# Selections of a Mamba scan by pairs of groups, four at once in four row tiles

## The chip, the core and the metric

The kernel runs on one core of one Trainium2 chip. The metric is the device time of one execution in microseconds (us); lower is better. A core has a matrix engine (PE), whose weight loads are a row of their own (PEld), a vector engine (DVE), an activation engine (ACT), a general engine (POOL) and a queue that starts transfers (SP). PE writes its results to PSUM, eight banks of 128 partitions by 512 float32. Everything here is float32, and the profile records each float32 matmul as two passes: two weight loads and two matmuls.

## The reference, cut to what matters

An image batch `x` of shape (4, 56, 56, 128) passes through four layers: windowed attention, a Mamba stage, an additive attention with a token-choosing expert layer, and a full attention with an expert layer. The change touches only the Mamba stage. It runs twice in a row (two blocks `l`) over each image row, a sequence of 56 tokens:

```python
xz = h @ in_w                          # 128 -> 512, split into u and res
u  = silu(causal_conv(u) + cb)         # 4 taps
dt, Bm, Cm = split(u @ xw)             # 8, 16, 16
delta = softplus(dt @ dtw + dtb)       # 256 channels
h_t = exp(delta * A) * h_{t-1} + delta * u * Bm      # 256 channels x 16 states
y_t = sum over states of h_t * Cm, plus u * D
out = (y * silu(res)) @ ow
```

## The kernel before, in words

The Mamba stage is `layer1`. It works in 56 blocks: 4 images, 7 chunks of 8 image rows (`CH` = 448 tokens), 2 layers `l`. A block has 256 channels with 16 states each, so 4096 recurrences; a group of 8 channels fills 128 partitions, and a block has 32 groups.

For each group `g` these steps are issued, on four engines:

- `decays(g)`: a matmul picks the 8 channels out of `delta`, repeats each over 16 states and scales by A (line 545). The operand is a half of 64 rows, so two such matmuls can lie in the array. The result is a PSUM tile `a` (three buffers), and ACT takes its exponential in place (line 548).
- `inputs(g)`: the same for `du` = delta * u with `pick` (line 555), into PSUM tile `u` (two buffers).
- `scan(g)`: DVE multiplies `u` by the spread B (`dBu`, line 562), then runs the recurrence along the 448 tokens into `hs` (line 566). After each odd group POOL multiplies the pair of `hs` by the spread C (`bc`), 128 x 896 (line 570).
- `sums(g)`: after every fourth group, four matmuls with 32 columns each add up the states into `y` (line 582). With the first of a half, a matmul with a diagonal of D begins `y` (line 577).

`gate(j, f)` multiplies a finished half of `y` by `silu(res)` (DVE, line 590); `project(j)` multiplies by `ow` (lines 598 and 611) and either copies the result to the next layer's `h` (ACT, line 604) or adds it to `x` (DVE, line 616).

While block j is scanned, `mamba_pre` issues the steps of block j+1, each after a given group: the convolution as 4 matmuls for each half (line 665) and its silu (line 672), the `res` matmuls (678) and their silu (685), `xproj` (691), a copy `dbl` (697), four `spread` matmuls (702), the softplus in parts on ACT, DVE and POOL (lines 711 to 736), and `du` on POOL (740). Their PSUM tile is `m` (two buffers).

The order is written out by hand: the context holds a manual schedule for PE, ACT, DVE and POOL, so every engine runs its instructions in the order in which Python issues them, and waits only for what its next instruction needs. The main loop is

```python
for g in range(GROUPS * len(order) + GROUPS // 2):
    ...
    scan(g)
    decays(g + 2)
    inputs(g + 1)
    if i % 4 == 3: sums(g - 7)
    if i == 4: gate(j - 1, 1)
    if i == 5: project(j - 1)
    if i == 20: gate(j, 0)
    for at, step in todo: ...   # steps of block j + 1 due after group i
```

Of the kernel before, what the change touches and what calls it, by code (L numbers as in the profile page):

```python
# [10 lines left out]
AF = mybir.ActivationFunctionType  # L11
ALU = mybir.AluOpType
AX = mybir.AxisListType
PSUM = bass.MemoryType.PSUM
# [3 lines left out]
B, HW, C = 4, 56, 128  # L18
S = HW * HW
P = 128  # L20
# [3 lines left out]
CH = TC * TP  # L24
# [12 lines left out]
QG, HR = 8, 64  # L37
GROUPS = DI // 8
# [18 lines left out]
def host_constants():  # L57

    j = np.arange(HW)
    start = np.clip(j - NB, 0, HW - KW)  # L60
    kj = j[:, None]
    inside = (kj >= start[None, :]) & (kj < start[None, :] + KW)
    toep = np.zeros((1 + KR, HW, HW), np.float32)
    toep[0] = np.where(inside, 0.0, NEG)
    for d in range(KR):
        toep[1 + d] = inside & (kj - j[None, :] + KW - 1 == d)
    group = np.kron(np.eye(32), np.full((4, 4), 0.25)).astype(np.float32)
    later = np.triu(np.ones((TP, TP), np.float32), 1)
    p = np.arange(P)
    place = np.zeros((P, QW + QW - JG), np.float32)  # L70
    place[p, QW - JG + p // AH] = 1.0


    pick = np.zeros((P, QG, P), np.float32)
    back = np.zeros((P, 4, HD), np.float32)
    for q in range(QG):
        pick[:, q, :] = (p % HR // 8 == q)[:, None] & (p[None, :] // DS == p[:, None] % 8)
    for q in range(4):
        back[p, q, 8 * q + p // DS] = 1.0
    return {  # L80
        "k_state": (p[None, :] % DS == np.arange(DS)[:, None]).astype(np.float32),
        "k_pick": pick.reshape(P, QG * P),
        "k_sum": back.reshape(P, 4 * HD),
        "k_toep": toep.reshape(1 + KR, HW * HW),
        "k_group": group,
        "k_later": later,
        "k_place": place,
    }


class Hybrid:
# [336 lines left out]

    def layer1_weights(self, wp):
# [15 lines left out]
        w["sum"] = self.load(wp, [P, 4, HD], "sum", a["k_sum"].rearrange("p (q c) -> p q c", q=4))  # L445
# [51 lines left out]
    def layer1(self):  # L497
# [5 lines left out]
        with ExitStack() as ctx:  # L503
# [4 lines left out]
            ps_m = ctx.enter_context(tc.tile_pool(name="l1_m", bufs=2, space=PSUM))  # L508
            ps_a = ctx.enter_context(tc.tile_pool(name="l1_a", bufs=3, space=PSUM))
            ps_u = ctx.enter_context(tc.tile_pool(name="l1_u", bufs=2, space=PSUM))  # L510
# [11 lines left out]
            ]  # L522
            h = {}
            pre, yg, A, U, HS, py = {}, {}, {}, {}, {}, {}
# [8 lines left out]
            def select(g):  # L533
                j, i = divmod(g, GROUPS)
                if j >= len(order):
                    return None
                half = slice(i % 2 * HR, (i % 2 + 1) * HR)
                return j, order[j][2], i // 16, i // 4 % 4 + 4 * (i // 2 % 2), half

            def decays(g):  # L540
                s = select(g)
                if s:
                    j, l, f, q, own = s
                    A[g] = self.t(ps_a, [P, 512], "a")[:, :CH]
                    nc.tensor.matmul(  # L545
                        A[g], w["A"][own, l, f, q, :], pre[j]["delta"][own, f], start=True, stop=True
                    )
                    nc.scalar.activation(A[g], A[g], AF.Exp)  # L548

            def inputs(g):  # L550
                s = select(g)
                if s:
                    j, l, f, q, own = s
                    U[g] = self.t(ps_u, [P, 512], "u")[:, :CH]
                    nc.tensor.matmul(  # L555
                        U[g], w["pick"][own, q, :], pre[j]["du"][own, f], start=True, stop=True
                    )

            def scan(g):
                j = g // GROUPS  # L560
                dBu = self.t(sm, [P, CH], "dBu")
                nc.vector.tensor_mul(dBu, U.pop(g), pre[j]["bc"][:, 0])  # L562
                if g % 2 == 0:
                    HS[g // 2] = self.t(sm, [P, 2, CH], "hs", bufs=6)
                hs = HS[g // 2]
                nc.vector.tensor_tensor_scan(  # L566
                    hs[:, g % 2], A.pop(g), dBu, 0.0, op0=ALU.mult, op1=ALU.add
                )
                if g % 2:
                    nc.gpsimd.tensor_mul(hs, hs, pre[j]["bc"][:, 1:2].to_broadcast([P, 2, CH]))  # L570

            def sums(g):

                j, l, f, q, _ = select(g)
                if q == 0:
                    py[j, f] = self.t(ps_y, [P, 512], "y")[:, :CH]
                    nc.tensor.matmul(
                        py[j, f], w["Dd"][:, l, f, :], pre[j]["us"][:, f], start=True, stop=False
                    )
                for r in range(4):  # L580
                    at = r % 2 * HR + r // 2 * HD
                    nc.tensor.matmul(  # L582
                        py[j, f][at : at + HD, :], w["sum"][:, q, :], HS[(g + r) // 2][:, r % 2],
                        start=False, stop=(q == 3),
                    )
# [36 lines left out]
            decays(0)  # L622
            decays(1)
            inputs(0)
            for g in range(GROUPS * len(order) + GROUPS // 2):
                j, i = divmod(g, GROUPS)
# [7 lines left out]
                if j < len(order):  # L634
                    scan(g)
                decays(g + 2)
                inputs(g + 1)
                if i % 4 == 3 and 0 <= g - 7 < GROUPS * len(order):
                    sums(g - 7)
                if i == 4 and j:  # L640
                    gate(j - 1, 1)
                if i == 5 and j:
                    project(j - 1)
                    pre.pop(j - 1)
                if i == 20 and j < len(order):
                    gate(j, 0)
                for at, step in todo:
                    if at == i:
                        step()

    def mamba_pre(self, pre, j, block, h, w, sm, m):
# [8 lines left out]
        def conv(f, k):  # L660
            if (f, k) == (0, 0):
                r["us"] = self.t(sm, [P, NHALF, CH], "us")
            if k == 0:
                ps[f] = m()[:, :CH]
            nc.tensor.matmul(  # L665
                seqs(ps[f]), w["in"][:, l, k, f * P : (f + 1) * P], h[b, c, l][:, :, k : k + HW],
                start=(k == 0), stop=(k == DC - 1),
            )

        def silu_u():  # L670
            for f in range(NHALF):
                nc.scalar.activation(r["us"][:, f], ps[f], AF.Silu, bias=w["cb"][:, l, f : f + 1])

        def res(f):
            if f == 0:
                r["sres"] = self.t(sm, [P, NHALF, CH], "sres")
            ps[f] = m()[:, :CH]
            nc.tensor.matmul(
                seqs(ps[f]), w["res"][:, l, f * P : (f + 1) * P], h[b, c, l][:, :, DC - 1 :],
                start=True, stop=True,  # L680
            )

        def silu_res():
            for f in range(NHALF):
                nc.scalar.activation(r["sres"][:, f], ps[f], AF.Silu)
# [13 lines left out]
        def spread(i):  # L699
            own = slice(i * HD, (i + 1) * HD)  # L700
            ps[i] = m()[:, :CH]
            nc.tensor.matmul(ps[i], w["dbl"][own, l, :], r["dbl"][own, :], start=True, stop=True)
# [3 lines left out]
        def parts():  # L706
            r["e"] = self.t(sm, [P, NHALF, CH], "sp_e", bufs=1)
            r["delta"] = self.t(sm, [P, NHALF, CH], "delta")
            for f in range(NHALF):
                dtb = w["dtb"][:, l, f : f + 1]  # L710
                nc.scalar.activation(r["e"][:, f], ps[f], AF.Abs, bias=dtb)
                nc.vector.tensor_scalar(r["delta"][:, f], ps[f], dtb, 0.0, op0=ALU.add, op1=ALU.max)
            nc.scalar.activation(r["e"], r["e"], AF.Exp, scale=-1.0)

        def copy_bc():
            r["bc"] = self.t(sm, [P, 2, CH], "bc")
            for i in range(2):
                nc.scalar.copy(r["bc"][:, i], ps[2 + i])
# [19 lines left out]
        def du():  # L738
            r["du"] = self.t(sm, [P, NHALF, CH], "du")
            nc.gpsimd.tensor_mul(r["du"], r["delta"], r["us"])  # L740
# [4 lines left out]
        steps = [(2 * i // 3, conv, i // DC, i % DC) for i in range(2 * DC)]  # L745
        steps += [
            (6, silu_u), (7, res, 0), (8, res, 1), (9, silu_res), (10, xproj, 0), (11, xproj, 1),
            (12, copy_dbl), (13, spread, 0), (13, spread, 1), (14, parts), (15, spread, 2),
            (15, spread, 3), (16, copy_bc), (16, one_plus), (17, log), (18, low), (20, log1p), (22, delta), (24, du),
# [405 lines left out]
```

## Time and profile before

| | us |
|---|---|
| median of 3 runs (11249.28 to 11265.89) | 11265.24 |
| the profiled execution | 11265.46 |
| its span, first to last instruction | 11263.7 |
| the Mamba scans, first to last start | 1097.8 to 4991.0 |
| PE busy in the span | 9968.8 (89%) |
| ACT busy | 6235.4 (55%) |
| DVE busy | 4399.8 (39%) |
| POOL busy | 2404.3 (21%) |
| PE busy, DVE busy in 3000 to 3500 | 412.81, 400.16 |
| granted PE clock: mean of the span; 3000 to 3500 | 0.933; 0.96 |

The scans take 3893 us, about 69.5 us for each of the 56 blocks. In that stage POOL is busy 291 to 298 us of 500 and ACT 231 to 239. Busy time of PE counts a stretch once in which several matmuls lie in the array, and the ends of matmuls are modelled, so it overstates how full PE is. The granted clock is what the throttle let PE have: 1.00 is full speed.

### The profile page before, as it was taken

To read this page: it belongs to the slowest core of one execution; us is meant where nothing else is said; L and a number is where in the kernel's file an instruction comes from. 1 tells how busy PE (TensorE), PEld (TensorE's weight loads), DVE (VectorE), ACT (ScalarE), POOL (GpSimd) and SP (SyncE) were. 2 spreads that over 40 slices of the span, in tenths; PEclk is the share of its full clock that TensorE was granted. 3 is DMA by queue.
4 is the path that set the end of the run, shared out by engine and by line. 5 is a ranking of instruction groups with operands and counts; after the bars stand their busy time and mean duration, and the time that the engine had idled before them with its cause. 6 is when DMAs were issued, how large, how long until landed. Compare 5 with 4: busy or idle time off the path is not lost.

```text
span 11263.7 us, 117588 instructions
## 1 busy us (share of the span) xinstructions
PE 9968.8 (89%) x45951; PEld 4111.7 (37%) x45951; DVE 4399.8 (39%) x8342; ACT 6235.4 (55%) x10930; POOL 2404.3 (21%) x1422
## 2 busy tenths in 40 slices
PE   7887888888888888879999999999999789898998
PEld 3443222222222222223333333333333387565655
DVE  3444877788788877880000000000000301304133
ACT  2222444444444444439998998999899502232322
POOL 0000655556565656640000000000000000000000
PEclk8887999999999999999999999999999758999999
DMA  1000000000000000000000000000000030000000
GB/s 38 1 1 10 1 1 1 1 1 1 1 1 1 1 1 1 1 1 1 1 1 1 1 1 1 1 1 1 1 1 1 16 105 3 6 1 6 1 6 6
DMA packets 90722, 61.48 MB, mean 5 GB/s; under 512 B 20635, under 2 KB 81587, under 8 KB 89971
## 3 DMA queue, kind: packets, MB, share of 16 engines
q1 hardware_dynamic: 90165, 53.96, 1.7%
q8 instruction: 361, 5.91, 0.2%
q14 instruction: 196, 1.61, 0.0%
HBM read 46.87 MB, written 7.07 MB: 5 GB/s over the span
## 4 chain that ended last, share of the span: by engine, by line
PE 75%; DVE 13%; ACT 9%; issue 2%; SPq 0%; POOL 0%; DMA 0%; DVEq 0%; ACTq 0%; POOLq 0%
PE s L833 26%; PE a L545 9%; PE o L1033 7%; PE s L1026 5%; DVE hs L566 5%; PE o L842 4%; PE m L665 3%; PE y L582 3%; DVE dBu L562 2%; ACT e L838 2%; PE d L408 2%; PE o L408 2%; PE s L391 2%; PE s L1103 1%; ACT a L548 1%
## 5 line engine op out<-in xcount | busy, mean ns | idle before, releaser
L828 ACT ACTIVATE th<-fT,g 128x448 f32<-128x448 f32 (+3 forms) x6272 | 3327.8, 621 | 17.6 <-DVE g L809 17.5
L833 PE MATMUL s<-th,place 128*32 128x448 f32 (+4 forms) x12544 | 3181.7, 516 | 7.0 <-ACT th L828 7.0
L545 PE MATMUL a<-delta,A_pick 64*128 64x448 f32 x3584 | 1878.7, 615 | 608.8 <-DVE hs L566 591.7
L570 POOL TENSOR_TENSOR hs<-hs,bc 128x896 f32<-128x896 f32 x896 | 1860.8, 2081 | 1409.4 <-DVE hs L566 1257.4
L548 ACT ACTIVATE a<-a 128x448 f32<-128x448 f32 x1792 | 936.3, 529 | 2024.1 <-PE u L555 1908.5
L566 DVE TENSOR_TENSOR_SCAN hs<-a,dBu 128x448 f32<-128x448 f32 x1792 | 1954.5, 1091 | 232.3 <-ACT a L548 30.2
L853 DVE TENSOR_SCALAR den<-o 112x1 f32<-112x1 f32 x224 | 31.8, 152 | 4961.3 <-PE o L842 3642.2
L555 PE MATMUL u<-du,pick 64*128 64x448 f32 x3584 | 1877.6, 615 | 0.0
L833 PEld LDWEIGHTS s<-th,place 128*32 128x32 f32 (+1 forms) x12544 | 787.1, 106 | 2129.8 <-ACT th L828 2030.4
L562 DVE TENSOR_TENSOR dBu<-u,bc 128x448 f32<-128x448 f32 x1792 | 1092.9, 610 | 430.6 <-PE u L555 420.9
L545 PEld LDWEIGHTS a<-delta,A_pick 64*128 64x128 f32 x3584 | 565.8, 193 | 1780.2 <-DVE hs L566 1246.8
L1031 ACT ACTIVATE e<-s,shift 112x448 f32<-112x448 f32 x784 | 495.4, 633 | 888.6 <-PE s L1026 840.4
L840 POOL TENSOR_TENSOR e<-e,later 112x112 f32<-112x112 f32 x112 | 47.2, 421 | 3813.8 <-ACT e L838 3813.8
L1033 PEld LDWEIGHTS o<-xa,e 112*112 112x112 f32 x6272 | 711.1, 176 | 297.7 <-ACT e L1031 295.5
L1033 PE MATMUL o<-xa,e 112*112 112x129 f32 x6272 | 789.3, 279 | 13.4 <-ACT e L1031 0.9
L1026 PE MATMUL s<-xT 128*112 128x448 f32 x1568 | 656.2, 541 | 0.0
L842 PE MATMUL o<-xa,e 112*112 112x129 f32 x3248 | 492.3, 288 | 105.9 <-ACT e L838 98.6
L555 PEld LDWEIGHTS u<-du,pick 64*128 64x128 f32 x3584 | 565.9, 193 | 54.4 <-issue 53.4
L842 PEld LDWEIGHTS o<-xa,e 112*112 112x112 f32 x3248 | 384.5, 176 | 446.7 <-ACT e L838 402.7
L396 ACT ACTIVATE e<-s 112x896 f32<-112x896 f32 (+1 forms) x272 | 206.2, 800 | 590.6 <-PE s L391 427.5
L582 PE MATMUL y<-hs,sum 128*32 128x448 f32 x3584 | 462.7, 589 | 4.0 <-POOL hs L570 4.0
L758 POOL MEMSET xa<- 112x28 f32 x12 | 1.6, 148 | 1823.6 <-DVE X L856 1281.6
(224 smaller groups left out, 8064.9 us busy)
## 6 DMA issues: line engine op xcount, KB each, us to landing
w<-in_L_ffn_weight SPq DMA_DIRECT2D x16, 1024.0 KB
w<-in_L_ffn_weight SPq DMA_DIRECT2D x64, 256.0 KB
X<-in_x SPq DMA_DIRECT2D x8, 784.0 KB
out<-X SPq DMA_DIRECT2D x8, 784.0 KB
e_edge<-dtab SPq DMA_DIRECT2D x42, 49.0 KB
cw<-in_L_conv_conv_w SPq DMA_DIRECT2D x1, 1024.0 KB
e_inner<-dtab SPq DMA_DIRECT2D x14, 49.0 KB
dtab<-tab SPq DMA_DIRECT2D x1, 637.0 KB
```

The source lines that it names most:

```text
L545: nc.tensor.matmul(A[g], w["A"][own, l, f, q, :], pre[j]["delta"][own, f], start=True, stop=True)
L548: nc.scalar.activation(A[g], A[g], AF.Exp)
L555: nc.tensor.matmul(U[g], w["pick"][own, q, :], pre[j]["du"][own, f], start=True, stop=True)
L562: nc.vector.tensor_mul(dBu, U.pop(g), pre[j]["bc"][:, 0])
L566: nc.vector.tensor_tensor_scan(hs[:, g % 2], A.pop(g), dBu, 0.0, op0=ALU.mult, op1=ALU.add)
L570: nc.gpsimd.tensor_mul(hs, hs, pre[j]["bc"][:, 1:2].to_broadcast([P, 2, CH]))
L582: nc.tensor.matmul(py[j, f][at : at + HD, :], w["sum"][:, q, :], HS[(g + r) // 2][:, r % 2], start=False, stop=(q == 3),)
L828: nc.scalar.activation(th[:, lo:], fT[:, c * CH + lo : (c + 1) * CH], AF.Tanh, bias=g[:, at : at + 1])
L833: nc.tensor.matmul(ps[QW * blk : QW * blk + rows, lo:CH], place[:, off : off + rows], th[:, lo:], start=(q == 0), stop=(n + 1 == NG or q = ...
L842: nc.tensor.matmul(po[s][:TP, : C + 1], e[:, s * TP : (s + 1) * TP], xa[:, J, :], start=(J == 0), stop=(J == TC * c + s),)
L1026: nc.tensor.matmul(ps[:TP, :CH], xT[:, t * TP : (t + 1) * TP], xT[:, c * CH : (c + 1) * CH], start=True, stop=True,)
L1033: nc.tensor.matmul(po[s][:TP, : C + 1], e[:, s * TP : (s + 1) * TP], xa[:, t, :], start=(t == 0), stop=(t == NT - 1),)
```

## The change

Two groups become a pair `p`, 16 pairs to a block.

- `select(p)` issues four matmuls one after the other, each on 32 rows: two for `a` (two groups, from `delta`) and two for `u` (from `du`). So that the four lie in four different row tiles, the halves of `du` are stored swapped: POOL writes `du` as two products over 64 partitions each.
- `a` and `u` are two banks each. `a` has two buffers (4 banks), `u` one (2), `m` one, `y` one: the eight banks.
- ACT takes one exponential over 128 x 896, DVE one product `dBu` over 128 x 896.
- DVE's order is: first scan of pair p, product of pair p+1, second scan of pair p.
- `sums` runs for two pairs at a time; the diagonal matmul is a step of its own, `skip`; `gate`, `project` and `skip` follow each other after pair 2, `gate` and `skip` after pair 10.
- `mamba_pre`: the convolution and `res` results are copied by ACT to a tile `raw`, and one silu over 128 x 1792 replaces four; `spread` evacuates each tile at once; the steps of a pair are issued half after `select`, half at the end.

```diff
-            ps_m = ctx.enter_context(tc.tile_pool(name="l1_m", bufs=2, space=PSUM))
-            ps_a = ctx.enter_context(tc.tile_pool(name="l1_a", bufs=3, space=PSUM))
-            ps_u = ctx.enter_context(tc.tile_pool(name="l1_u", bufs=2, space=PSUM))
+            ps_m = ctx.enter_context(tc.tile_pool(name="l1_m", bufs=1, space=PSUM))
+            ps_a = ctx.enter_context(tc.tile_pool(name="l1_a", bufs=2, space=PSUM))
+            ps_u = ctx.enter_context(tc.tile_pool(name="l1_u", bufs=1, space=PSUM))
...
+            def place(p):
+                j, i = divmod(p, PAIRS)
+                return j, i // 8, i // 2 % 4, i % 2 * 2
+
+            def select(p):
+                if p >= n_pairs:
+                    return
+                j, f, q, r0 = place(p)
+                l = order[j][2]
+                A[p] = self.t(ps_a, [P, 2, 512], "a")[:, :, :CH]
+                U[p] = self.t(ps_u, [P, 2, 512], "u")[:, :, :CH]
+                for k in range(2):
+                    own = slice((r0 + k) * HD, (r0 + k + 1) * HD)
                     nc.tensor.matmul(
+                        A[p][:, k], w["A"][own, l, f, q, :], pre[j]["delta"][own, f],
+                        start=True, stop=True,
+                    )
+                for k in range(2):
+                    r = (r0 + k + 2) % 4
+                    own = slice(r * HD, (r + 1) * HD)
                     nc.tensor.matmul(
+                        U[p][:, k], w["pick"][own, q, :], pre[j]["du"][own, f], start=True, stop=True
+                    )
+                nc.scalar.activation(A[p], A[p], AF.Exp)
+
+            def inputs(p):
+                if p < n_pairs:
+                    V[p] = self.t(sm, [P, 2, CH], "dBu")
+                    nc.vector.tensor_mul(
+                        V[p], U.pop(p), pre[p // PAIRS]["bc"][:, 0:1].to_broadcast([P, 2, CH])
+                    )
+
+            def scan(p, k):
+                if k == 0:
+                    HS[p] = self.t(sm, [P, 2, CH], "hs", bufs=5)
                 nc.vector.tensor_tensor_scan(
+                    HS[p][:, k], A[p][:, k], V[p][:, k], 0.0, op0=ALU.mult, op1=ALU.add
+                )
...
-                if j < len(order):
-                    scan(g)
-                decays(g + 2)
-                inputs(g + 1)
-                if i % 4 == 3 and 0 <= g - 7 < GROUPS * len(order):
-                    sums(g - 7)
-                if i == 4 and j:
+                now = [x for x in todo if x[0] // 2 == i]
+                if p < n_pairs:
+                    scan(p, 0)
+                select(p + 1)
+                for _, step in now[: len(now) // 2]:
+                    step()
+                inputs(p + 1)
+                if p < n_pairs:
+                    scan(p, 1)
+                    weigh(p)
+                if i % 2 and 0 <= p - 3 < n_pairs:
+                    sums(p - 3)
+                if i == 2 and j:
                     gate(j - 1, 1)
-                if i == 5 and j:
                     project(j - 1)
                     pre.pop(j - 1)
-                if i == 20 and j < len(order):
+                if i == 2 and j < len(order):
+                    skip(j, 0)
+                if i == 10 and j < len(order):
                     gate(j, 0)
+                    skip(j, 1)
+                for _, step in now[len(now) // 2 :]:
+                    step()
...
+        def silu():
+            act = self.t(sm, [P, 2 * NHALF, CH], "act")
+            r["us"], r["sres"] = act[:, 0:NHALF], act[:, NHALF:]
+            nc.scalar.activation(act, r["raw"], AF.Silu)
...
             r["du"] = self.t(sm, [P, NHALF, CH], "du")
-            nc.gpsimd.tensor_mul(r["du"], r["delta"], r["us"])
+            for k in range(2):
+                to, of = slice(k * 64, k * 64 + 64), slice(64 - k * 64, 128 - k * 64)
+                nc.gpsimd.tensor_mul(r["du"][to], r["delta"][of], r["us"][of])
...
-        steps = [(2 * i // 3, conv, i // DC, i % DC) for i in range(2 * DC)]
+        steps = [(2 * i // 3, project, i // DC, i % DC) for i in range(2 * DC)]
         steps += [
-            (6, silu_u), (7, res, 0), (8, res, 1), (9, silu_res), (10, xproj, 0), (11, xproj, 1),
-            (12, copy_dbl), (13, spread, 0), (13, spread, 1), (14, parts), (15, spread, 2),
-            (15, spread, 3), (16, copy_bc), (16, one_plus), (17, log), (18, low), (20, log1p), (22, delta), (24, du),
+            (6, project, 2, 0), (7, project, 3, 0), (8, silu), (9, xproj, 0), (10, xproj, 1),
+            (11, copy_dbl), (12, spread, 0), (13, spread, 1), (14, exp), (15, one_plus),
+            (16, log), (17, low), (18, spread, 2), (19, spread, 3), (19, log1p), (21, delta), (23, du),
         ]
```

In the new `mamba_pre`, `project(f, k)` is the convolution's tap k of half f (f below 2) or the `res` matmul (f of 2 and 3), followed by ACT's copy to `raw` when the tile is whole. `spread(i)` for i below 2 is followed at once by ACT's absolute value and by DVE's `tensor_scalar` (the line 712 of before), for i of 2 and 3 by ACT's copy to `bc`.

## The prediction

> **What bounds the kernel now.** First the windows by stage: of 500 us in the scans PE is busy 413 and DVE 400, so neither is full.
>
> ```profile
> 3000.00:3500.00 500.00, 412.81 (x1734) 130.03 (x1732) 400.16 (x496) 238.41 (x378) 297.37 (x162) 0.97 0.00 1
> ```
>
> (PE, PEld, DVE, ACT, POOL, granted clock.) Then the groups by line in that window, for durations and what ended idle time:
>
> ```profile
> L566 DVE TENSOR_TENSOR_SCAN hs<-a,dBu 128x448 f32<-128x448 f32 x232 | 253.0, 1091 | 30.4 <-ACT a L548 3.6 <-DVE dBu L562 1.0 <-ACT sp_ln L726 0.5
> L545 PE MATMUL a<-delta,A_pick 64*128 64x448 f32 x464 | 239.8, 606 | 73.8 <-DVE hs L566 73.1
> L562 DVE TENSOR_TENSOR dBu<-u,bc 128x448 f32<-128x448 f32 x232 | 141.5, 610 | 55.8 <-PE u L555 54.6
> ```
>
> PE waits for scans to free `a`, DVE for `u`: a ring between two engines. Scan starts in the trace lie 1.71 to 1.74 us apart where DVE alone limits; the median plain block takes 68.5 us, so some 13 of it are waits and other DVE work. The timeline gives one turn of the ring at full clock, then one at half:
>
> ```profile
> 2511.33 0.64 PE L545 MATMUL a<-delta,A_pick 64*128 64x448 f32 x1
> 2511.33 0.64 PE L555 MATMUL u<-du,pick 64*128 64x448 f32 x1
> 2511.81 0.54 PE L545 MATMUL a<-delta,A_pick 64*128 64x448 f32 x1
> 2512.42 0.62 DVE L562 TENSOR_TENSOR dBu<-u,bc 128x448 f32<-128x448 f32 x1
> ```
> ```profile
> 2528.45 1.11 PE L555 MATMUL u<-du,pick 64*128 64x448 f32 x1
> 2529.35 0.95 PE L555 MATMUL u<-du,pick 64*128 64x448 f32 x1
> 2530.38 0.62 DVE L562 TENSOR_TENSOR dBu<-u,bc 128x448 f32<-128x448 f32 x1 [0.28 <-PE u L555]
> ```
>
> From selection to product: 1.10 us at full clock, 1.94 at half. The clock changes in steps of 3.41 us; windows of that length show when:
>
> ```profile
> 2736.67:2740.09 3.42, 2.70 (x18) 0.76 (x16) 3.21 (x4) 3.38 (x4) 1.60 (x1) 1.00 0.02 5
> 2740.09:2743.50 3.41, 1.61 (x8) 0.30 (x4) 2.81 (x4) 2.65 (x5) 2.07 (x2) 1.00 0.01 2
> 2743.50:2746.91 3.41, 2.94 (x8) 1.01 (x8) 2.92 (x5) 0.53 (x1) 3.41 (x2) 0.50 0.00 0
> 2746.91:2750.33 3.42, 3.42 (x12) 0.70 (x10) 2.46 (x3) 0.53 (x1) 3.42 (x3) 0.50 0.01 2
> 2750.33:2753.74 3.41, 2.22 (x14) 0.79 (x10) 1.87 (x3) 1.06 (x2) 3.41 (x3) 1.00 0.00 0
> ```
>
> PE is busy 1.61 of 3.41: the next window has half clock. 2.94 doesn't end that, 3.42 does. I cut the whole scan stage so: of 67 full-clock windows with PE busy under half, 66 were followed by half clock; of 971 above, 12. Of 79 half-clock windows busy over 0.9, 77 were followed by full clock; of 23 below, 1. Before, 9% of windows are at half clock.
>
> **The parts.** *Four in the array.* A selection with what follows holds PE 0.94 us (starts 2510.377 back to 2509.424 and the like). Whether four row tiles run together, layer 0 shows: four 32-row score matmuls (line 391) start at 94.915, 94.921, 94.935 and 94.941, and second passes follow 0.42 later. So four cost 0.94, like two; per block PE sheds 16 x 0.94 = 15 us. [...]
>
> *DVE.* Two products of 0.599 become one of 896: from 0.467 at 0.96 elements/ns and 0.132 fixed, 1.07 us (bounds 0.95 and 1.22, two whole ones: 16 x 0.12 to 0.15 = 2 us a block). A product followed by its own scan has the scan 0.70 to 0.73 later, though it lasts 0.60; a scan lets the next go after 1.01. Alternated, nothing follows its own input, so DVE alone would need 1.01 + 0.98 + 1.01 = 3.00 for a pair, against 2 x 1.72 = 3.44.
>
> *The ring.* `a` has two buffers of a pair, so selection p+1 waits for the second scan of p-1, and product p+1 follows it in the same pair. A pair costs 1.10 (selection to product) + 0.98 (product) + 1.09 (second scan) + 0.05 (semaphore, 2512.34 to 2512.39) = 3.22; the first scan lies under the selection. At half clock 4.06. Sixteen pairs: 51.5.
>
> *What lies between.* PE is in order, so what is issued in a pair beyond its 3.22 delays the next selection. Durations: a matmul between others 0.95, following one of its kind 0.75, `sums` 0.89, `project` 1.93 or 1.70.
> - Pairs 0 and 1, convolution: 0.94 + 2.45 = 3.39, and 0.94 + 0.95 + 0.89 + 1.70 = 4.48: +1.4.
> - Pair 2: `gate` 0.65, `project` 2.04 until `x` can be added, 0.69, `skip` 0.95, convolution 0.75, all before the next selection, with one `y` bank: 5.1 in place of 0.13: +5.0 (+4.6 where ACT copies `h`). Next scan, product and exponential are queued behind it. Pair 3, `res`: +0.5.
> - Pair 4: `xproj` waits for the silu, and selection 6 behind it: 1.06 to the exponential, 0.95, table 1.28, silu 1.80 (0.951 + 2 x 0.42, from the 448 and 896 rows), 0.95: 6.0 against 3.22: +2.8.
> - Pairs 6 and 7: two `delta` operations on DVE 1.2 and a wait for `spread` 0.7: +1.9.
> - Pairs 8 and 9: exponential, table, log, identity, table, exponential (1.06 + 0.95 + 1.28 + 0.95 + 0.94 + 1.28 + 0.95), `bc` copy 0.54, `spread` 0.95 for the one `m` bank: 9.0 against 6.4: +2.5.
> - Pair 10: `gate` and `skip`: +1.5.
>
> Sum 15.4; the block 67.0 at full clock, 1.5 below 68.5. Costed at nothing: two table loads fewer (6 to 4) and four copies more, since ACT is busy 238 of 500; the two `du` products on POOL, 1.04 to 2.08 us each (2.08 for 896 columns): queued behind `weigh` they end some 3 us before selection 16 and the sums of pair 15 need POOL's results, and if that cover is gone cost at most 2.08 x 56 = 116 us; three image changes (84 to 86 us blocks) with one `m` bank, 0 to 3 x 16 = 48 us, nearer 0 as DVE does most of that work.
>
> *The clock.* A plain pair now holds PE 1.03 (recorded span of a selection) and every second pair 0.96 more: 0.32 to 0.62 of 3.22, mostly under a half where before it was 1.03 of 1.71. At half clock it is about 0.7 of 4.06, under the 0.9 that ends it. Charges per block:
> - pairs 11 to 15: 5 x 0.84, a quarter off for windows that happen to return: 3.2;
> - pairs 0 and 1 begin at half clock and need one dense window, some 5 us, in which half the work is lost: 2.5, take 2.0;
> - PE idles 4 us for the silu; then `xproj`, selection, `xproj`, `sums` at half: 2.9, take 2.5;
> - pair 8 has only a selection: 1.1 in pairs 9 and 10; the `gate` wait of pair 2: 0.5.
>
> 9.3 in all (13.4 with every charge in full), so 76.3 a block, 7.8 over 68.5. The granted clock of the stage falls from 0.95 to about 0.77. [...]
>
> **Sum.** Profiled 11265.5 (span 11263.7 and 1.8 around it; the median is 11265.24): + 56 x 7.8 = 437: 11,702, say 11,700. With half the charges 71.6 a block: 11,440; with all in full 80.4: 11,930.
>
> **Rivals.** *The clock stays (faster).* If four tiles at once count as more activity than two, or selections fall so that windows hold over half, the block is 67.0: 56 x 1.5 = 84 less, 11,181; with the 0.95 product 11,080. It decides while charges stay under 1.5 us a block, two pairs at half clock. For it: 91% of windows are full now. Against: 66 of 67. Chance 0.17; within 0.2% (22.5 us, about what a measurement can tell) 0.05, the edge between the two.
> *Row tiles don't overlap.* If `a` and `u` pairs take turns, the selection is 0.75 longer, a pair 3.97 at full clock; PE then stays above half: 67.0 + 12 = 79.0, +588: 11,850. Against: line 391. Chance 0.06.
> *DVE's alternation gains nothing* because the ring, not DVE, sets the pair: that is in my sum. Forecast, slower by the clock: 0.72.
>
> The numbers: faster 0.17, same 0.05, slower 0.78. The likeliest case alone spans 11,440 to 11,930; the range reaches down to 11,160, into the full-clock case, since without it 0.22 and more would be left out.
>
> **What would show it.** Right: scan-stage clock 0.70 to 0.85, plain pairs 4.06 apart with selections 1.9 before their product, PE busy well under 413 of 500, 5 us without a scan after pair 2. Wrong: clock at 0.95 and pairs at 3.2 (first rival); four selections starting in two steps (second); a product far from 1.07.

## The result, and the profile after

The changed kernel takes 12010.55 us (median of 4 runs, 12006.2 to 12014.64) against 11264.95 for the kernel before (4 runs): a ratio of 1.0665, 95% interval 1.0647 to 1.0684, so 746 us slower. The prediction had the side and the mechanism, but its 11,700 was too low and its range, up to 11,930, too short. The profiled execution took 12006.2 (span 12004.4). Of the 741 us by which it is longer than the one of before, 720 lie between the first and the last scan start: 4612.8 us (1127.5 to 5740.2) in place of 3893.1. The median block is 81.9 us.

The granted clock in the page's slices (tenths of full speed, 40 slices), then the 500 us window that was shown of before (us, PE, PEld, DVE, ACT, POOL, clock, DMA, GB/s):

```profile
PEclk8887766666666666666899999999999956999999
```
```profile
3000.00:3500.00 500.00, 363.47 (x1442) 114.82 (x1434) 318.20 (x340) 184.86 (x212) 257.10 (x140) 0.68 0.00 1
```

The clock of the stage is 0.68; in the same 500 us before it was 0.97, as the row in the prediction has it. Every engine that does the stage's work does less of it in the same time: DVE runs 189 scans here, before 232. The groups by line in that window (count | busy, mean ns of one | idle before, by releaser):

```profile
L569 DVE TENSOR_TENSOR_SCAN hs<-a,dBu 128x448 f32<-128x448 f32 x189 | 197.4, 1073 | 0.5
L547 PE MATMUL a<-delta,A_pick 32*128 32x448 f32 x380 | 150.4, 847 | 66.8 <-DVE hs L569 66.0 <-DVE gn_var L189 0.7
...
L562 DVE TENSOR_TENSOR dBu<-u,bc 128x896 f32<-128x896 f32 x95 | 103.4, 1088 | 145.0 <-PE u L554 133.4 <-PE a L547 11.6
```

The scan itself no longer waits (0.5 us): DVE's idle time has moved to the product, 145.0 us in 95 turns, nearly all of it for `u`, and PE for its part waits for scans. A matmul lasts 847 ns on average, before 606. The timeline shows two turns of the ring, the first at half clock and the second at full (start, us, instruction):

```profile
3085.39 1.11 PE L547 MATMUL a<-delta,A_pick 32*128 32x448 f32 x2 [2.32 <-DVE hs L569]
...
3085.41 1.12 PE L554 MATMUL u<-du,pick 32*128 32x448 f32 x2
...
3087.35 1.09 DVE L562 TENSOR_TENSOR dBu<-u,bc 128x896 f32<-128x896 f32 x1 [1.13 <-PE u L554]
...
3088.36 2.06 DVE L569 TENSOR_TENSOR_SCAN hs<-a,dBu 128x448 f32<-128x448 f32 x2
...
3089.59 0.65 PE L547 MATMUL a<-delta,A_pick 32*128 32x448 f32 x2 [0.80 <-DVE hs L569]
...
3089.60 0.64 PE L554 MATMUL u<-du,pick 32*128 32x448 f32 x2
...
3090.70 1.09 DVE L562 TENSOR_TENSOR dBu<-u,bc 128x896 f32<-128x896 f32 x1 [0.28 <-PE u L554]
3091.71 2.06 DVE L569 TENSOR_TENSOR_SCAN hs<-a,dBu 128x448 f32<-128x448 f32 x2
...
3092.93 1.11 PE L547 MATMUL a<-delta,A_pick 32*128 32x448 f32 x2 [2.32 <-DVE hs L569]
```

All four first passes start within 0.02 us, so four row tiles do run together. From selection to product it is 1.96 us at half clock and 1.11 at full, and the turns are 4.20 (3085.39 to 3089.59) and 3.34 us long. Then the same stretch by windows of 3.41 us, with the clock behind the busy times (the cuts lie 0.2 us behind the clock's own steps, hence 0.53 and 0.97):

```profile
3081.92:3085.33 3.41, 1.16 (x8) 0.00 (x0) 2.29 (x4) 0.90 (x1) 3.33 (x2) 0.50 0.00 0
3085.33:3088.75 3.42, 3.36 (x16) 0.74 (x16) 2.29 (x3) 0.90 (x1) 3.30 (x5) 0.53 0.02 5
3088.75:3092.16 3.41, 1.07 (x12) 0.34 (x8) 3.13 (x4) 0.90 (x1) 3.08 (x2) 0.97 0.00 0
3092.16:3095.57 3.41, 2.63 (x16) 0.75 (x16) 2.29 (x3) 0.69 (x1) 2.07 (x1) 0.50 0.00 0
3095.57:3098.99 3.42, 2.75 (x17) 0.60 (x9) 2.39 (x3) 0.21 (x1) 1.86 (x1) 0.50 0.00 0
3098.99:3102.40 3.41, 3.41 (x7) 1.70 (x6) 3.07 (x3) 0.90 (x1) 1.27 (x2) 0.53 0.00 0
3102.40:3105.81 3.41, 3.41 (x21) 0.80 (x19) 1.70 (x2) 1.54 (x2) 1.02 (x1) 1.00 0.00 0
```

A window that happens to be nearly full (3.36) gives one window at full clock; in that one PE is busy only 1.07, and the clock is lost again. 2.63 and 2.75 don't bring it back; only the convolution's row of six matmuls (3098.93) does. Cut so, 63% of the windows of the stage are at half clock, before 9%. After full-clock windows busy under half, 240 of 240 fell; over 0.7, none of 222. Of 350 half-clock windows busy 0.7 to 0.9, 330 stayed. One band does not fit the rule that was read from the kernel before: of full-clock windows busy 0.5 to 0.7, 32 of 35 fell here and 12 of 235 before. So busy time alone does not sort these windows; the last section has a count that sorts them better.

Three waits of PE that aren't the ring's stand out, in the waits of PE from 1300 to 4400 us (total, times, longest), and in PE's timeline behind pair 4, behind pair 10 and, in the next block, behind pair 2:

```profile
PE a L547 <- DVE hs L569: 407.6, 293, 4.2
PE m L701 <- ACT act L695: 153.7, 38, 4.0
PE y L589 <- DVE yg L596: 105.9, 37, 3.4
...
PE y L604 <- DVE yg L596: 36.0, 19, 1.9
PE y L617 <- DVE yg L596: 34.1, 18, 1.9
```
```profile
3045.35 1.86 PE L701 MATMUL m<-act,xw 128*128 128x448 f32 x2 [4.04 <-ACT act L695]
3047.14 1.12 PE L547 MATMUL a<-delta,A_pick 32*128 32x448 f32 x2
...
3075.23 1.83 PE L589 MATMUL y<-act,D_diag 128*128 128x448 f32 x2 [2.85 <-DVE yg L596]
...
3098.93 4.12 PE L685 MATMUL m<-h,in_w 128*128 128x448 f32 x6
...
3111.36 2.29 PE L604 MATMUL y<-yg,ow 128*128 128x448 f32 x4 [1.89 <-DVE yg L596]
3114.27 1.86 PE L589 MATMUL y<-act,D_diag 128*128 128x448 f32 x2 [0.63 <-ACT h L610]
```

`xproj` (L701) waits 4.04 us for the silu, with the next selection queued behind it, and then both run at half clock. That is what the prediction said of pair 4. The second is `skip` (L589) behind the gate of pair 10: it waits 2.85 us for the one `y` bank and runs at half clock, as does the selection behind it. The third is `project` (L604 and L617) and `skip` behind the gate of pair 2.

### The profile page after: what moved, and what is told of

Read it like the earlier page. It is cut to its first block, busy times and chain, and to the rows that moved or that the text cites. A ratio compares the mean times of both kernels' runs of the same rounds, so it can differ in the third digit from the quotient of the medians.

```text
span 12004.4 us, 117322 instructions
## 1 busy us (share of the span) xinstructions
PE 10131.5 (84%) x45951; PEld 4135.5 (34%) x45951; DVE 4198.8 (35%) x7430; ACT 6119.8 (51%) x9980; POOL 2527.2 (21%) x1478
## 4 chain that ended last, share of the span: by engine, by line
PE 75%; DVE 15%; ACT 7%; issue 3%; SPq 0%; POOL 0%; DMA 0%; ACTq 0%; DVEq 0%; POOLq 0%
PE s L844 24%; PE a L547 10%; PE o L1044 7%; DVE dBu L562 5%; PE s L1037 5%; DVE hs L569 5%; PE m L685 4%; PE o L853 4%; ACT e L849 2%; PE y L581 2%; PE y L589 2%; PE m L701 2%; PE d L406 2%; PE o L406 2%; PE m L712 1%
## 5 line engine op out<-in xcount | busy, mean ns | idle before, releaser
L547 PE MATMUL a<-delta,A_pick 32*128 32x448 f32 x3584 | 1421.7, 845 | 629.4 <-DVE hs L569 618.4
L569 DVE TENSOR_TENSOR_SCAN hs<-a,dBu 128x448 f32<-128x448 f32 x1792 | 1868.9, 1073 | 5.6
L557 ACT ACTIVATE a<-a 128x896 f32<-128x896 f32 x896 | 808.2, 902 | 2079.1 <-PE u L554 2057.7
L562 DVE TENSOR_TENSOR dBu<-u,bc 128x896 f32<-128x896 f32 x896 | 976.0, 1089 | 1455.6 <-PE u L554 1334.3
L554 PE MATMUL u<-du,pick 32*128 32x448 f32 x3584 | 1382.5, 861 | 0.0
L547 PEld LDWEIGHTS a<-delta,A_pick 32*128 32x128 f32 x3584 | 421.3, 259 | 1585.5 <-issue 1225.8
L581 PE MATMUL y<-hs,sum 128*32 128x448 f32 x3584 | 644.1, 803 | 2.8 <-POOL hs L575 2.8
L701 PE MATMUL m<-act,xw 128*128 128x448 f32 x224 | 207.1, 1029 | 226.1 <-ACT act L695 226.1
L712 PE MATMUL m<-dbl,dbl_w 32*128 32x448 f32 x448 | 306.5, 775 | 96.8 <-DVE delta L720 88.3
```

What stands on the lines that cost most here:

```text
L547: nc.tensor.matmul(A[p][:, k], w["A"][own, l, f, q, :], pre[j]["delta"][own, f], start=True, stop=True,)
L554: nc.tensor.matmul(U[p][:, k], w["pick"][own, q, :], pre[j]["du"][own, f], start=True, stop=True)
L557: nc.scalar.activation(A[p], A[p], AF.Exp)
L562: nc.vector.tensor_mul(V[p], U.pop(p), pre[p // PAIRS]["bc"][:, 0:1].to_broadcast([P, 2, CH]))
L569: nc.vector.tensor_tensor_scan(HS[p][:, k], A[p][:, k], V[p][:, k], 0.0, op0=ALU.mult, op1=ALU.add)
L581: nc.tensor.matmul(py[j, f][r * HD : (r + 1) * HD, :], w["sum"][:, q, :], HS[p + r // 2][:, r % 2], start=False, stop=(q == QG - 1),)
```

## The experiments

The theory after this result: the ring of two `a` buffers leaves PE mostly idle, so the clock halves and stretches what lies in the ring, and waits in PE's queue come on top. Rivals: the time is the order's alone (the ring and the waits, whatever the clock); or four small tiles are slow by themselves. Pitches below are medians from the first scan of a pair to that of the next, so a wait behind pair 4 shows in the pitch of pair 5. A plain pair is one in which hardly more than the selection is issued, as 12 to 15.

**Fillers in the change** (e1_fill). Matmuls whose result nobody reads, in a free `m` tile, so many at the end of the given pair of a block (in pairs 9 and 10 right behind the selection):

```
+FILL = {4: 4, 7: 2, 8: 2, 9: 1, 10: 2, 11: 1, 12: 2, 13: 1, 14: 2, 15: 1}
...
+            def fill(p, n):
...
+                    ps = m()
+                    for _ in range(n):
+                        nc.tensor.matmul(
+                            ps[:, :CH], w["Dd"][:, 0, 0, :], pre[j]["us"][:, 0], start=True, stop=True
+                        )
```

> The changed kernel with filler matmuls (128x128 by 448, into a free m tile that nobody reads) where PE idles: 4 behind pair 4's selection while xproj waits for the silu, 1 or 2 in pairs 7 to 15; some 18 per block, 16 us of added PE work. Clock theory (half clock is what the time is lost to): the stage's granted clock rises from 0.68 to over 0.9, plain pairs fall from 4.20 to 3.2-3.3 us, the block from 81.9 to 67-70 us, the whole to 11,180-11,350 us. Ring theory (the chain selection, product, scan with two buffers is slow by itself and the clock is a side effect): clock may rise, the whole stays above 11,700 us. If the fillers only stand in the way: at or above 12,010.

Measured: 11472.09 us, 1.0188 of before (1.0171 to 1.0205), 538 under the change. Clock of the stage 0.934, block 71.4, pairs 12 to 15 at 3.35. More work on PE made the kernel 538 us faster: the clock is most of the 746. It is less than expected, since fillers also stand in the way: pairs 7 and 8 take 3.50 and 4.84 on average where 3.00 and 3.35 are possible.

**The same with 8 columns** (e5_fill8), the control for the order: as many instructions, but with hardly any work.

```
-                            ps[:, :CH], w["Dd"][:, 0, 0, :], pre[j]["us"][:, 0], start=True, stop=True
+                            ps[:, :8], w["Dd"][:, 0, 0, :], pre[j]["us"][:, 0, 0:8], start=True, stop=True
```

> The control for the fillers: the same number of filler matmuls in the same places with the same waits, but 8 columns in place of 448, so PE is hardly busier. Clock theory: granted clock of the stage 0.67-0.71 and 11,950-12,080 us, as the changed kernel. Theory that the fillers help by shifting the order or the waits: about 11,470 us, as with full fillers.

Measured: 11987.51 us, 1.0638 (1.0617 to 1.066), clock 0.688. The 500 us windows of e1_fill and of e5_fill8:

```profile
3000.00:3500.00 500.00, 414.56 (x1848) 142.54 (x1852) 357.14 (x378) 198.28 (x230) 291.56 (x161) 0.92 0.00 1
```
```profile
3000.00:3500.00 500.00, 399.03 (x1666) 150.89 (x1666) 321.73 (x343) 186.36 (x213) 257.70 (x140) 0.68 0.00 1
```

With 448 columns the clock of the stage is 0.934, with 8 it is 0.688, the change's own 0.68. So it is what PE does, not where an instruction stands. It isn't the recorded busy time either: 399 and 415 us of 500 are close, since the fillers of 8 columns are recorded too (224 passes more than the change has in this window, 36 us more busy).

**Fillers in the kernel before** (e6_before_fill): seven a block, after groups 17, 21, 22, 25, 26, 29 and 30.

```
+                if i in (17, 21, 22, 25, 26, 29, 30) and j < len(order):
+                    nc.tensor.matmul(
+                        m()[:, :CH], w["Dd"][:, 0, 0, :], pre[j]["us"][:, 0], start=True, stop=True
+                    )
```

> The kernel before with 7 fillers per block (128x128 by 448) behind its sparse groups 17 to 30. It shows what the clock costs before. Clock theory, from the clock of 0.955 there and from a scan that mostly covers the selection: clock over 0.97, at most 1 us per block less, 11,200-11,270 us. If the clock were as dear there as in the changed kernel (10 us per block for 0.25 of clock): 11,160 us.

Measured: 11228.74 us, 0.9964 (0.9949 to 0.9978), clock 0.992. Fillers bring the kernel before 38 us (11266.41 in the same runs), and the change 538.

**Every selection twice** (e2_twice), into the same tiles:

```
+                for _ in range(2):
+                    for k in range(2):
...
+                        nc.tensor.matmul(
+                            A[p][:, k], w["A"][own, l, f, q, :], pre[j]["delta"][own, f],
```

> The changed kernel with every selection issued twice into the same tiles: 16 x 0.75 to 0.94 us more PE work per block at full clock, all of it on the ring between scan and product. Clock theory: PE is busy over half of every window, the clock returns, a plain pair is 3.2 + 0.75 = about 4.0 us at full clock against 4.20 now: whole time 11,850-12,150 us, about unchanged although the selections double. Theory that the clock doesn't matter (the selection's own length counts, at the clock of 0.68): 16 x 1.1 us more per block, 12,900-13,100 us.

Measured: 12378.71 us, 1.0992 (1.097 to 1.1014), clock 0.842: between the two expectations. In the plain pairs the clock theory held: they take 4.10 at full clock where the change takes 4.19 at half, so twice the selection costs nothing there. But pairs 5, 6 and 11, where PE waits for other reasons and the clock still halves at times (0.78, 0.86 and 0.61 on average), went from 7.71, 6.37 and 5.97 to 8.43, 7.06 and 7.46. Work in the ring's own path was a poor filler here.

**`u` selected a pair earlier** (e3_early), apart from `a`, so that the product no longer waits for the selection behind the scan:

```
+            def select_u(p):
...
                 inputs(p + 1)
+                select_u(p + 2)
```

> The changed kernel with u of pair p+2 selected right after the product of pair p+1, apart from a: two tiles at a time, 16 x 0.94 us more PE work per block, and the product no longer waits for a selection of its own pair. Clock theory and ring theory both say faster here: plain pairs at 3.0 us (DVE alone), clock over 0.9, block 63-68 us, the whole 10,950-11,250 us. If four row tiles at once were what carries the change, taking them apart costs: over 12,010 us.

Measured: 12622.9 us, 1.1209 (1.1186 to 1.1231), clock 0.618. A clear miss. With `a` and `u` no longer together only two row tiles work at a time, and in PE's timeline they take turns with everything else:

```profile
3133.20 1.86 PE L560 MATMUL u<-du,pick 32*128 32x448 f32 x4 [1.97 <-DVE dBu L567]
3134.99 1.72 PE L586 MATMUL y<-hs,sum 128*32 128x448 f32 x8
3136.64 2.56 PE L546 MATMUL a<-delta,A_pick 32*128 32x448 f32 x8
3138.30 1.70 PE L560 MATMUL u<-du,pick 32*128 32x448 f32 x4
```

PE is busy 423 of 500 us, more than the 363 of the change, yet the clock is lower. Pairs 12 and 14 take 4.94 and 5.53; 13 and 15 take 2.99, the 3.00 that the prediction added up for DVE alone. That a busy PE stayed at half clock was not in my rule; e11_moved_two returns to it. With one buffer of `u`, the edit also puts a wait for the product into PE's queue (1.97 us in the first line), so what the two tiles alone cost isn't shown here.

**`xproj` one pair later** (e4_xlate), to give the silu its time:

```
-            (6, project, 2, 0), (7, project, 3, 0), (8, silu), (9, xproj, 0), (10, xproj, 1),
-            (11, copy_dbl), (12, spread, 0), (13, spread, 1), (14, exp), (15, one_plus),
+            (6, project, 2, 0), (7, project, 3, 0), (8, silu), (10, xproj, 0), (11, xproj, 1),
+            (12, copy_dbl), (12, spread, 0), (13, spread, 1), (14, exp), (15, one_plus),
```

> The changed kernel with xproj one pair later (both in pair 5), so that selection 6 isn't queued behind a matmul that waits for the silu. If the silu wait and the half clock after it cost what the walk said (2.8 + 2.9 us per block): 11,690-11,800 us. If the wait only moves to the next pair: 11,950-12,030 us.

Measured: 11949.3 us, 1.061 (1.0589 to 1.0632), clock 0.683. Pair 5 fell from 7.71 to 4.20 and pair 6 rose from 6.37 to 11.38: `xproj`, the copy of `dbl` and two `spread` now wait for each other within one pair. Moved alone, this wait only became the next one: 61 us came of it.

**The waits taken apart** (e7_moved, and with fillers e8_moved_fill). Each step that waits is issued after the next selection, and what its result needs a pair later: `project` in pair 3 with the addition to `x` or the copy of `h` at the pair's end, the two `skip` in pairs 4 and 11, the silu at the end of pair 5, `xproj` in pair 7, and each `spread` in a pair of its own with its evacuation at the end. `hs` has six buffers in place of five, and the taps of the convolution and the steps that bring a new image are spread differently over the pairs. Its core:

```
                 select(p + 1)
+                if i == 3 and j:
+                    keep = project(j - 1)
+                if i == 4 and j < len(order):
+                    skip(j, 0)
+                    sums(p - 4)
+                if i == 11 and j < len(order):
+                    skip(j, 1)
+                fill(p, FILL.get(i, 0))
+                for at, step in now:
+                    if at % 2 == 0:
+                        step()
...
+            (8, project, 2, 0), (10, project, 3, 0), (11, silu), (14, xproj, 0), (14, xproj, 1),
+            (15, copy_dbl), (16, spread, 0), (17, taken, 0), (18, spread, 1), (19, taken, 1),
+            (19, exp), (19, one_plus), (20, spread, 2), (21, taken, 2), (21, log), (21, low), (21, log1p),
+            (22, spread, 3), (22, delta), (23, taken, 3), (24, du),
```

`FILL` is empty in e7_moved; in e8_moved_fill it is `{6: 2, 8: 1, 10: 1, 12: 2, 13: 1, 14: 2, 15: 1}`.

> The changed kernel without fillers, with its waits taken apart: project a pair after its gate, skip and the sums behind it a pair after that, res, silu, xproj and spread each in a later pair than what they wait for, spread's evacuation at the end of the pair. Ring and waits theory: these waits are 15 us per block at full clock, so 11,300-11,600 us. Clock theory: less waiting leaves PE idle in other places, the clock stays at 0.65-0.72 and plain pairs at 4.2 us: 11,500-11,900 us.

> The same with fillers in pairs 6, 8, 10 and 12 to 15 (10 per block). Both causes taken away: clock over 0.92, plain pairs 3.2-3.4 us, block 58-65 us, the whole 10,650-11,050 us, faster than both kernels. If four tiles and pairs can't pay even so: over 11,265 us.

Measured: 11005.07 us, 0.9767 (0.9747 to 0.9786), clock 0.788, block 64.0; with fillers 10906.9 us, 0.9681 (0.9666 to 0.9695), clock 0.971, block 61.2. Both beat the kernel before. With fillers it is as expected; without, both theories were too slow (11,300 to 11,600 and 11,500 to 11,900 us), and the clock came out above the 0.65 to 0.72 of the second. So the four tiles and the alternation of DVE can pay; as put in place, their order and the clock took more than they gave. The 500 us window of e8_moved_fill has DVE at 419 busy, before 400:

```profile
3000.00:3500.00 500.00, 423.43 (x2104) 136.72 (x2096) 419.30 (x431) 248.04 (x285) 354.77 (x191) 1.00 0.00 1
```

| us | no fillers | fillers | they bring |
|---|---|---|---|
| waits as in the change | 12010.6 | 11472.1 | 538 |
| waits taken apart | 11005.1 | 10906.9 | 98 |
| taking them apart brings | 1005 | 565 | |

Waits and clock aren't two separate sums in this table: taking the waits apart brings 440 us less once fillers stand in the kernel. Behind a wait the timelines show matmuls at half clock, as `xproj` with 1.86 us for its two passes after its 4.04 us (1.02 in the kernel before, at full clock); without fillers a wait here costs itself and that. (The two sets of fillers differ, 18 and 10 a block, and the table carries that too.)

**Each half of that alone**: only `project`, `skip` and `sums` moved (e9_project), and only the steps of the next block and of a new image (e10_steps). Both have the sixth `hs` buffer.

```
-                    project(j - 1)
-                    pre.pop(j - 1)
-                if i == 2 and j < len(order):
-                    skip(j, 0)
...
-                    skip(j, 1)
```
```
-            (6, project, 2, 0), (7, project, 3, 0), (8, silu), (9, xproj, 0), (10, xproj, 1),
...
+            (8, project, 2, 0), (10, project, 3, 0), (11, silu), (14, xproj, 0), (14, xproj, 1),
```

> The changed kernel with only project, skip and the sums behind it moved (project a pair after its gate, skip a pair after that; skip of the second half a pair after its gate). In the changed kernel the pairs around them (2, 3, 10, 11) take 25.6 us, in the kernel with all waits moved 15.4. If each wait costs by itself: some 8-10 us per block less, 11,450-11,560 us. If the waits are lost only together (the clock falls for the next one anyway): above 11,750 us.

> The changed kernel with only the steps of the next block moved (convolution, res, silu, xproj, spread, softplus), project and skip as in the changed kernel. Its pairs 5 and 6 take 14.1 us, with all moved 8.6; pairs 0 and 1 9.2 against 6.8. Each by itself: 7-8 us per block less, 11,560-11,620 us; only together: above 11,750 us.

Measured: 11446.33 us, 1.0156 (1.0126 to 1.0185), clock 0.753; and 11215.04 us, 0.9961 (0.9938 to 0.9983), clock 0.798. They bring 564 and 796, together 1360 where both at once bring 1005. In e9_project pair 3 falls from 8.65 to 3.12. In e10_steps pairs 5 and 6 fall from 14.08 together to 8.00, and pair 3 too, to 6.29, though `project` stays where it was; pairs 0 and 1 go back to 3.35 and 3.43, the full clock. So part of the gain is had by either edit alone; what the sixth `hs` buffer gives, which both have, was not measured by itself. e9_project ends just under its 11,450. e10_steps is some 350 us faster than expected: my price left out that its steps also decide the clock of pairs they don't stand in.

**Two tiles at once in place of four** (e11_moved_two): e7_moved with `du` written unswapped by one product, so that `a` and `u` need the same two row tiles.

```
-                    r = (r0 + k + 2) % 4
+                    r = r0 + k
...
-            for k in range(2):
-                to, of = slice(k * 64, k * 64 + 64), slice(64 - k * 64, 128 - k * 64)
-                nc.gpsimd.tensor_mul(r["du"][to], r["delta"][of], r["us"][of])
+            nc.gpsimd.tensor_mul(r["du"], r["delta"], r["us"])
```

> The kernel with all waits moved, without fillers, and with du unswapped in one product, so that a and u lie in the same two row tiles: two at once, not four, 0.75 us more per selection on the ring, and one POOL product less. If four tiles at once pay: plain pairs 4.0-4.1 us at full clock, 11,350-11,500 us. If what the four tiles save is lost again to the clock (0.79 in the stage with four, then over 0.9 with two): 10,950-11,100 us.

Measured: 12292.34 us, 1.0906 (1.0874 to 1.0938), 1287 over e7_moved; clock 0.664, plain pairs 5.63. Four at once do pay. The size was far off, because I expected the busier PE to get its clock back. In PE's timeline `a` and `u` take turns, and the windows (columns as above) stay at half clock though PE is full:

```profile
3099.33 1.86 PE L548 MATMUL a<-delta,A_pick 32*128 32x448 f32 x4 [2.19 <-DVE hs L570]
3100.98 1.70 PE L555 MATMUL u<-du,pick 32*128 32x448 f32 x4
```
```profile
3102.41:3105.83 3.42, 3.42 (x14) 0.61 (x11) 3.04 (x4) 1.59 (x2) 0.84 (x1) 0.50 0.00 0
3105.83:3109.24 3.41, 3.41 (x9) 1.77 (x10) 0.81 (x2) 1.85 (x2) 1.24 (x1) 0.50 0.00 0
...
3112.65:3116.07 3.42, 3.42 (x8) 0.87 (x4) 1.39 (x3) 3.36 (x4) 2.37 (x2) 0.50 0.00 0
3116.07:3119.48 3.41, 3.41 (x11) 0.70 (x10) 1.79 (x2) 1.14 (x2) 3.25 (x3) 0.50 0.01 2
```

## Why the prediction was right, and where it was not

**The mechanism** stands. The ring sets the plain pairs (e1_fill, e2_twice), the four tiles leave PE too little work in it, and the clock falls for that (0.934 in e1_fill against 0.688 in e5_fill8). That busy time measures this work was wrong in general, as the last section shows; for the plain pairs it gave the right side. The first rival, that the clock stays, needed charges under 1.5 us a block; they were some 11.8. The second, that row tiles don't overlap, is out: four start within 0.02 us, and from `u`'s first matmul to the product it is 1.114 us in the median at full clock where two tiles of 64 rows took 1.090: a difference of 0.02.

**The step that failed** is the sum, by two terms. I compare means over the 52 blocks that bring no new image, since means add up: 68.8 us before, 81.6 after, so +12.8 where I had +7.8.

*The clock's charges*: 9.3 predicted. The pairs of the change less those of e1_fill (pairs 7 and 8 against 3.00 and 3.35, as fillers stand there) give:

| us a block | predicted | measured |
|---|---|---|
| pairs 0 and 1, begun at half clock | 2.0 | 2.1 |
| after the `gate` wait, pairs 2 and 3 | 0.5 | 1.35 |
| the silu and after, pairs 4 to 6 | 2.5 | 2.2 |
| pairs 7 to 10 | 1.1 | 2.0 |
| pairs 11 to 15 | 3.2 | 4.2 |
| sum | 9.3 | 11.85 |

In the last row the quarter off for windows that happen to return was right for the plain pairs: 12 to 15 paid 0.81, 0.81, 0.07 and 0.84, together three quarters of 4 x 0.84, as pair 14 is back at full clock in 48 of 56 blocks. (The median block, 81.92 us, is 24 windows of 3.413 us, so the pairs tend to keep their place in the windows.) What I had too small is pair 11: 1.68, twice 0.84, for the `skip` that waits for pair 10's gate and then runs at half clock with the selection behind it; among the clock's charges I had none for that wait. In the row above I charged what follows pair 8 but not pair 8 itself (0.84). And I charged pair 2's `gate` with its wait only, not with the `project` and `skip` that follow at half clock. The 13.4 "with every charge in full" isn't the sum of my list, which in full is 11.2, and 13.4 is 16 x 0.84; the measured 11.85 lies above the whole list, so it was charges that were missing, and not their discount. The stage clock came out at 0.68, below the 0.70 to 0.85 that I had named. The clock was lost without an idle window: in none of those shown above is PE idle throughout, and after 1.07 busy of 3.41 the next had 0.50.

*The block at full clock*: 67.0 predicted, 1.5 under before. e1_fill's mean, 71.8, less 2.0 for its fillers in pairs 7 and 8 is 69.8, 1.0 over before. The same 69.8 by four pairs each, against 3.22 a pair and what I had put between:

| us a block | predicted | e1_fill, so corrected |
|---|---|---|
| pairs 0 to 3 | 19.6 | 20.9 |
| pairs 4 to 7 | 17.6 | 18.7 |
| pairs 8 to 11 | 16.9 | 16.8 |
| pairs 12 to 15 | 12.9 | 13.4 |
| sum | 66.9 | 69.8 |

In the last row it is the ring: a plain turn takes 3.35 and not 3.22. Selection to product is 1.117 and not 1.10, the product lets the second scan start after 1.008 and not 0.98, and the next selection starts 1.225 after that scan and not 1.14: the whole 0.13. Pairs 0 to 7 are 2.4 over, more than 8 x 0.13; there the steps between the turns cost more than I had put down, and the four fillers of pair 4 may have a part in it. Which of them it is stays open. That the clock in e1_fill is 0.934 and not 1 leaves some of the 69.8 to the clock; I can't part it.

Together 2.5 from the clock and 2.5 from the block are the missing 5.0, some 280 of the 304 us by which the profiled execution exceeds its forecast.

**What was right besides**: the product 1.09 us (1.07 predicted, with 0.96 elements a ns, which line 400 of before shows: 268 ns for 112 columns and 618 for 448); DVE alone 2.98 a pair (3.00), reached only in pair 7; the plain pair at half clock 4.19 (4.06); 6.6 us between the two scans of pair 3, behind pair 2's `project`, where 5 without a scan were predicted; blocks that change the image 99.7, so 18 over the others, about as before (16), which had been left at nearly nothing.

**What I didn't see**: that the waits could be had apart. I priced them as part of the change, but the two-by-two shows that they are as large as the clock's share, and that one feeds the other.

## What to carry to other kernels

Where a ring with other engines sets the pace, look at PE's clock before you count on matmuls that fill less of the array: here it went from 0.97 to 0.68 in the same 500 us, and a plain pair took 4.19 us at half clock where e1_fill's took 3.35. Cut the trace into windows of the length that its clock records have (3.413 us here), and see which of them are followed by half clock: by busy time, and by the count of the next section. Where a queue runs in the order of issue, as PE's does here (the selection stood behind `xproj`'s wait of 4.04 us), issue a step that waits after the next piece of the main loop and not ahead of it, and move all steps of such a chain together: `xproj` moved alone brought 61 us, all waits taken apart 1005. Then see whether the clock still needs a filler; in e8_moved_fill it brought 98 us.

## What the chip showed that was not expected

- Matmuls nobody reads made a kernel 538 us faster (e1_fill); the same with 8 columns in place of 448 brought 23 (e5_fill8).
- Busy time alone doesn't sort the windows. In e11_moved_two, with two 32-row tiles at once, 593 half-clock windows were busy over 0.9, and 81% of them stayed at half clock; before 2 of 79 did, and in the change 49 of 302. A count that I fitted to these traces sorts them better. Take each recorded pass of a matmul as its columns times the part of the 128x128 array that its tile fills (a quarter for 32x128 and for 128x32, a half for 64x128), spread it over its recorded time, and add up each window of 3.413 us, the length of the trace's own clock records. In the scan stages of the kernel before and of the change windows above 1560 were followed by full clock and windows below by half, whichever clock they had themselves, with 11 errors in 2488. In the runs e1_fill to e11_moved_two the same 1560 is wrong for 204 of 13,787 windows; sorting by busy time as it was read from the kernel before (half at full clock, 0.9 at half) is wrong for 2527 of them. A half-clock window of before that is busy throughout (from 2746.9 us) comes to 1835, one of e11_moved_two (from 3106.0) to 909. The 1560 is an estimate from these traces alone, and no run varied the filled part by itself: how the chip sets its clock is not shown.
- By this count four 32-row tiles at once are no more than two of 64 rows. The selections of a pair came to 4 x 2 x 448 / 2 = 1792 before and come to 4 x 2 x 448 / 4 = 896 now; with the 448 of `sums` (896 every second pair) a plain pair of the change has 1344 in 3.35 us, under 1560, where before it had 2240 in 3.44. A filler adds 896, one of 8 columns 16.
- Two selections one after the other cost no more than one: 4.10 us a plain pair, at full clock (e2_twice), against 4.19 at half in the change.
